# Two adaptive-norm transformer blocks: RMS scaling on another engine, a shorter Newton step, and a later start for the last batches' states

## The chip, the core and the metric

The kernel runs on one core of a Trainium2 chip. A core has five engines, each of which works through its own queue in order: TensorE (PE) for matrix products, with its weight loads (PEld), VectorE (DVE), ScalarE (ACT), GpSimd (POOL) and SyncE (SP), which starts most of the transfers. The metric is the device time in microseconds; before, three runs gave 1119.42, 1120.37 and 1123.93 us, median 1120.37.

## The reference, cut to what matters

The input is 8 sequences of 512 tokens by 128 channels. Block 0 is an attention with 16 heads and then a mixture of eight experts with two chosen per token. Block 1 is a state-space layer and then a second mixture with a small feed-forward. Each half is preceded by a layer norm, scaled and shifted by rows from a modulation, and followed by a gated residual. The change lies in block 1:

```
# state-space layer: depthwise convolution, projection, a scan over 512 tokens
xc    = conv(x) + conv_b
proj  = xc @ Win + b_in                      # delta, B_in, C for 16 states
A_bar = exp(softplus(delta) * A)
h     = scan(A_bar, B_bar)                   # h_t = A_bar_t h_{t-1} + B_bar_t
y     = C * h @ Wout + b_out

# second mixture: all experts, gates that are zero outside the top two
x1       = x + silu(pointwise(causal_conv(x)))
rw       = gates of the two largest logits of x1
ye       = silu(x1 @ expert_w[e] + expert_b[e])           # e = 0..7
r        = x1 + (sum_e rw[e] * ye[e]) @ out_w + out_b
h        = norm_w * (r / sqrt(mean(r * r) + 1e-6))        # RMS norm
out      = h + gelu(h @ ff_down_w + ff_down_b) @ ff_up_w + ff_up_b
```

The 512 tokens of a sequence ("batch" b below) are held as four tiles of 128 tokens.

## The kernel before, in words

The kernel has three phases in one program. Attention runs slot by slot for all batches. Then block 0's mixture runs as a list of n = 62 blocks of 256 tokens (work, lines 1460 to 1464): routed tokens, and the shared expert for everyone. Under these blocks, and then after them, runs block 1.

Block 1's order is written out by hand. when(t, function, arguments) at line 829 puts a call at step t; while blocks are left, one step runs per block, and after them the steps from n on follow each other at once. A step is no time, it is a place in the order: what is issued at a lower step, or at the same step but registered earlier, comes first in the queue of each engine. Every instruction is pinned to that order, so one that waits holds up all that is behind it on its engine.

The steps that matter:

- **States.** The batches go through the state-space layer in groups 0 to 3, 4 and 5, 6 and 7 (GROUPS, line 1131). gather (line 972) fetches the mixture's rows with POOL's indirect transfers; combine (986) adds them with the gates, on DVE; two_stats, ssm_root, ssm_centre, ssm_channels and ssm_conv make the convolved channels; ssm_project (1167) makes the inputs of the states; chain_1 to chain_4 (1195 to 1232) are the state arithmetic of a whole group, with exponentials and a logarithm on ACT, four operations on POOL (da, ts) and the scan on DVE; out_weights (1234) and ssm_out (1241) bring the result back to the tokens.
- **Lead-in.** lead_in (1495) takes one batch from ssm_out through the second layer norm (ffn_root, ffn_centre), ffn_channels, ffn_pointwise, ffn_logits and the choice of two experts (ffn_ranks, ffn_chosen, ffn_tanh, ffn_gates) to ffn_gates_out. There PE transposes the gates, and SP writes them to memory, from where ffn_spread (1341) loads them, repeated over the partitions, as gb. In ffn_ranks POOL multiplies the tie mask rk_eq, on which ffn_chosen waits.
- **Experts.** base[b] (1506) is the step of batch b's first expert, eight steps a batch. At base[b] + e expert_in multiplies (PE) and applies SiLU (ACT, ye); three steps later expert_gate multiplies with the gate (DVE, t), and for some e POOL adds two or four such t; expert_sum (1393) then multiplies by out_w into r.
- **RMS norm.** rms_squares on ACT, rms_root on DVE and POOL, where a power of -1/2 gives a first root; rms_scale (1410) refines the root with one Newton step, root_end (326), and makes h; rms_turn (1417) transposes h, copies it to h2t and makes two small factors for ff_up: diag, the gate of the residual on a diagonal, and the gated feed-forward weights up (in the profile futg). root_end serves the layer norms too.
- **End.** ff_down (1429, with Gelu) and ff_up (1436) for batches 0 to 3, 4 to 6, and 7; ff_up also adds the residual on DVE and starts the output's transfer.

norm_row (1035) spreads the norm's weight over the partitions once, as the row nw that rms_scale uses. It runs at step 11. The scheduling lines that the change moves are 1506, 1530 and 1571 to 1590.

Of the kernel before, what the change touches and what calls it, by code (L numbers as in the profile page):

```python
# [10 lines left out]
FP = mybir.dt.float32  # L11
I32 = mybir.dt.int32
U32 = mybir.dt.uint32
AF = mybir.ActivationFunctionType
ALU = mybir.AluOpType
# [3 lines left out]
B, S, D = 8, 512, 128  # L19
P = 128  # L20
NC4 = S // P
NT = B * NC4
NE, NF = 8, 4
# [45 lines left out]
def tile_adaln_two_blocks(  # L69
# [21 lines left out]
    V, A, G, T, Q = nc.vector, nc.scalar, nc.gpsimd, nc.tensor, nc.sync  # L91

    const = ctx.enter_context(tc.tile_pool(name="const", bufs=1))
    stat = ctx.enter_context(tc.tile_pool(name="stat", bufs=4))
# [3 lines left out]
    def ct(shape, name):  # L98
        return const.tile(shape, FP, tag=name, name=name)
# [10 lines left out]
    ident = ct([P, P], "ident")  # L110
# [29 lines left out]
    fut_sb = ct([32, D], "fut_sb")  # L140
# [4 lines left out]
    def col(name, i=0, n=1):  # L145
        a = COLS[name][0] + i
        return pc[:, a : a + n]
# [34 lines left out]
    mpads = []  # L182
# [10 lines left out]
    mod1 = ct([P, 6, B], "mod1")  # L193
# [5 lines left out]
    with tc.tile_pool(name="ps0", bufs=3, space=PSUM) as ps0:  # L199

        def p0():
            return ps0.tile([P, 4, P], FP, tag="p0", name="p0")
# [3 lines left out]
        for layer, mod in ((0, mod0), (1, mod1)):  # L206
            pm = p0()
            pmv = pm.rearrange("p a b -> p (a b)")
            for k in range(6):
                T.matmul(  # L210
                    pmv[:, 8 * k : 8 * k + 8],
                    lhsT=wmod_sb[:, layer, k * D : (k + 1) * D],
                    rhs=sc_t[:, 8 * layer : 8 * layer + 8],
                    start=True,
                    stop=True,
# [29 lines left out]
        for src, dst in rows:  # L245
            for b0 in range(0, B, 4):
                pg = p0()
# [67 lines left out]
    def root_begin(r, var, eps, scale=None, on=None):  # L315

        on = on or V
        v = stat.tile([P, NC4], FP, tag="var4", name="var4")
        if scale is None:
            on.tensor_scalar(v, var, eps, None, ALU.add)  # L320
        else:
            on.tensor_scalar(v, var, scale, eps, ALU.mult, ALU.add)
        G.tensor_tensor(r, v, mhalf, ALU.pow)
        return v

    def root_end(r, v, on=None):

        on = on or V
        on.tensor_tensor(v, v, r, ALU.mult)
        on.tensor_tensor(v, v, r, ALU.mult)  # L330
        on.tensor_scalar(v, v, -0.5, 1.5, ALU.mult, ALU.add)
        on.tensor_tensor(r, r, v, ALU.mult)


    dram = ctx.enter_context(tc.tile_pool(name="rows", bufs=1, space=bass.MemoryType.DRAM))
# [17 lines left out]
    pin = tc.keep_in_program_order  # L353
    V, A, G, Q = (InOrder(e, pin) for e in (V, A, G, Q))
# [3 lines left out]
    with tc.tile_pool(name="at", bufs=2) as at, tc.tile_pool(name="sc", bufs=4, space=PSUM) as psc, tc.tile_pool(  # L358
        name="mx", bufs=2, space=PSUM
# [13 lines left out]
        def bank(name):  # L373
            return psc.tile([P, NC4, P], FP, tag="sc", name=name)

        def flat(ps):
            return ps.rearrange("p c t -> p (c t)")
# [451 lines left out]
        def when(t, do, *args):  # L829
            events.setdefault(t, []).append(lambda: do(*args))  # L830

        def lt(shape, name, tag=None, bufs=1):
            return lw.tile(shape, FP, tag=tag or name, name=name, bufs=bufs)
# [179 lines left out]
        k1 = {}  # L1013
# [18 lines left out]
            V.tensor_scalar(g, mod1[:, k, :], col(c), None, ALU.mult)  # L1032
            row_tiles(g, fours(dst))

        def norm_row():
            pg = bank("pnw")
            pin(T.matmul(pg[:, 0, :], lhsT=col("norm_w").to_broadcast([P, P]), rhs=ident, start=True, stop=True))
            k1["nw"] = lt([P, D], "nw")
            A.copy(k1["nw"], pg[:, 0, :])

        def states_1():

            rep = lt([16, 8, 16], "rep")
            V.tensor_copy(rep, ident[0:16, 0:16].unsqueeze(1).to_broadcast([16, 8, 16]))
            pr = flat(bank("prep"))
            pin(
                T.matmul(
                    pr[:, 0 : 6 + D], lhsT=rep.rearrange("n b m -> n (b m)"), rhs=ssm_sb, start=True, stop=True
                )
            )  # L1050
            sr = k1["sr"] = lt([P, 6 + D], "sr")
            V.tensor_copy(sr, pr[:, 0 : 6 + D])
            hm = lt([P, 2], "hm")
            V.tensor_reduce(hm, ident.rearrange("p (s h n) -> p h s n", h=2, n=16), AX.XY, ALU.add)
            wop = k1["wop"] = lt([P, 2, D], "wop")
            for h in range(2):
                V.tensor_scalar(wop[:, h, :], sr[:, 6:], hm[:, h : h + 1], None, ALU.mult)

            bias = k1["bias"] = lt([P, 3], "sbias")
            V.tensor_copy(bias[:, 0:1], sr[:, 1:2])  # L1060
            V.tensor_add(bias[:, 1:3], sr[:, 2:5:2], sr[:, 3:6:2])
            V.tensor_scalar(bias[:, 1:3], bias[:, 1:3], 0.5, None, ALU.mult)
            wip = k1["wip"] = lt([P, 3, 2, 32], "wip")
            V.memset(wip, 0.0)
            for h in range(2):
                c = slice(16 * h, 16 * h + 16)
                V.tensor_copy(wip[:, 0, h, c], win_sb[:, 0:16])
                for k in (1, 2):
                    two = win_sb[:, 32 * k - 16 : 32 * k + 16].rearrange("p (n two) -> p n two", two=2)
                    V.tensor_add(wip[:, k, h, c], two[:, :, 0], two[:, :, 1])  # L1070
                    V.tensor_scalar(wip[:, k, h, c], wip[:, k, h, c], 0.5, None, ALU.mult)
# [336 lines left out]
            f["v"] = root_begin(f["rr"], f["ss"], 1e-6, 1.0 / D)  # L1408

        def rms_scale(b):  # L1410
            f = ffn[b]
            root_end(f["rr"], f["v"])
            h2 = f["h2"] = ek.tile([P, NC4, D], FP, tag="h2", name="h2", bufs=1)
            for c in range(NC4):
                V.scalar_tensor_tensor(h2[:, c, :], f["r"][:, c, :], f["rr"][:, c : c + 1], k1["nw"], ALU.mult, ALU.mult)

        def rms_turn(b):
            f = ffn[b]
            pt = bank("ph2")
            for c in range(NC4):  # L1420
                pin(T.transpose(pt[:, c, :], f["h2"][:, c, :], ident))  # L1421
            f["h2t"] = flat(lt([P, NC4, D], "h2t", tag="sh", bufs=B))
            A.copy(f["h2t"], flat(pt))
            f["diag"] = ek.tile([P, D], FP, tag="diag", name="diag", bufs=4)
            V.tensor_scalar(f["diag"], ident, mod1[:, 5, b : b + 1], None, ALU.mult)
            f["up"] = ek.tile([32, D], FP, tag="futg", name="futg", bufs=4)
            V.tensor_tensor(f["up"], fut_sb, mpads[b // 4][0:32, b % 4, :], ALU.mult)

        def ff_down(b):
            f = ffn[b]  # L1430
# [33 lines left out]
        n = len(work)  # L1464
# [10 lines left out]
        when(13, row_tiles, mod0[:, 5, :], fours(sb_rows))  # L1475
        when(14, scaled_rows, 5, "ff_up_b", cb_rows)
        when(10, row_tiles, mod1[:, 5, :], mpads[0:2])
        when(11, norm_row)
        when(23, states_1)
        when(26, states_2)  # L1480
        when(28, pointwise)
# [2 lines left out]
        def later(t, us):  # L1484
            while us > 0:
                us -= 4.0 if t < n else 2.2
                t += 1
            return t

        def chain(h, t, lags):  # L1490
            steps = ((chain_1, 0), (chain_1, 1), (chain_2, 0), (chain_2, 1), (chain_3, 0), (chain_3, 1), (chain_4,))
            for (do, *args), i in zip(steps, lags):
                when(t + i, do, h, *args)

        def lead_in(b, t):

            when(t, ssm_out, b)
            for i in range(2):
                when(later(t, 2 * i + 1) if t >= n else t, two_stats, b, mv4, i)
            for do, us in (  # L1500
                (ffn_root, 4), (ffn_centre, 8), (ffn_channels, 12), (ffn_pointwise, 16), (ffn_logits, 22),
                (ffn_ranks, 24), (ffn_chosen, 28), (ffn_tanh, 30), (ffn_gates, 32), (ffn_gates_out, 36),
            ):
                when(later(t, us), do, b)

        base = [n + 5 + NE * b for b in range(B)]
        for b in range(B):
            t = base[b]
            for e in range(NE):
                when(t + e, expert_in, b, e)  # L1510
        for b in range(B):
            t = base[b]
# [14 lines left out]
            when(late + (4 if b < last else 3), rms_scale, b)  # L1527
            when(late + (6 if b < last else 4), rms_turn, b)

        for bs, t in ((range(4), base[3] + 20), (range(4, 7), base[6] + 20), ((7,), base[7] + 16)):  # L1530
            for b in bs:
                when(t, ff_down, b)
                when(t + 1 + (b - bs[0]), ff_up, b)
# [34 lines left out]

        for k in range(2 * PC[1]):
            when(n - 2 + k // 3, gather, PB[0] + k // 8, k % 8)  # L1570
        when(n, out_weights, 1)
        chain(1, n, (0, 1, 2, 4, 6, 7, 8))
        lead_in(4, n + 10)
        lead_in(5, n + 13)
        for b, t in ((6, n + 1), (7, n + 4)):
            for c in range(NC4):
                when(t + c, combine, b, c)
            when(t + 4, combine, b, NC4)
            for i in range(2):
                when(t + 5 + i, two_stats, b, mv3, i)  # L1580
                when(t + 12 + i, ssm_conv, b, i)
            when(t + 7, ssm_root, b)
            when(t + 9, ssm_centre, b)
            when(t + 10, ssm_bias, b)
            when(t + 11, ssm_channels, b)
        when(n + 16, out_weights, 2)
        when(n + 19, ssm_project, 2, 0)
        chain(2, n + 20, (0, 1, 2, 4, 6, 7, 8))
        lead_in(6, n + 30)
        lead_in(7, n + 37)  # L1590


        LAST = 2 * STEPS + 8
# [36 lines left out]
        ek = ek_cm.__enter__()  # L1630
# [70 lines left out]
```

## Time and profile before

The profiled execution took 1124.82 us in all, its span from first to last instruction is 1123.0 us, and the mean granted clock of TensorE is 0.943 of full speed.

| Engine | busy, us | share of the span |
|---|---|---|
| PE | 1024.6 | 91% |
| PEld | 668.8 | 60% |
| DVE | 665.2 | 59% |
| ACT | 634.2 | 56% |
| POOL | 470.6 | 42% |

A busy time is a sum of instruction spans. Attention ends near 580 us, the mixture of block 0 near 900 us, and the experts of block 1 fill the rest. Most operations of DVE, ACT and POOL carry the same line, 65, as a helper issues them; they are told apart by the tiles they write and read (out<-in). Rows of the parts that the change touches, over the whole execution:

| Operation | engine | count | median, ns |
|---|---|---|---|
| h<-r,rr,nw (128x128) | DVE | 32 | 343 |
| diag<-ident,mod (128x128) | DVE | 8 | 278 |
| futg<-fut_sb,mpad (32x128) | DVE | 8 | 273 |
| sq<-r (128x128, from PSUM) | ACT | 32 | 278 |
| h2t<-ph (128x512, mean) | ACT | 8 | 582 |
| ACT_TABLE_LOAD (mean) | ACT | 17 after 740 us | 1283 |
| rr<-var,mhalf (128x4) | POOL | 8 | 1392 |
| t<-t (128x512) | POOL | 34 | 1270 |
| wo<-wqk,ga_rows (128x128) | POOL | 8 | 457 |
| yg<-y_rows,yrows (gather; mean) | POOL | 64 | 980 |

### The profile page before, as it was taken

How to read it: one execution, taken by the hardware profiler on the slowest of the kernel's cores; microseconds unless marked ns; L12 is line 12 of the kernel's file. 1: busy time of each engine (PE TensorE's matmuls, PEld its weight loads, DVE VectorE, ACT ScalarE, POOL GpSimd, SP SyncE). 2: the span in 40 equal slices, each digit the busy share in tenths (PEclk: the TensorE clock that was granted, in tenths of full speed). 3: DMA queues.
4: the chain of work that ended last, by engine and by line, in shares of the span. 5: the costliest groups of instructions: out<-in, count | busy, mean ns of one | idle time of the engine just before them, and what ended most of it. 6: DMA issues, size and time to landing. Idle time of an engine off the chain costs nothing. (4 is left out here: it accounts for less than half of the span.)

```text
span 1123.0 us, 24186 instructions
## 1 busy us (share of the span) xinstructions
PE 1024.6 (91%) x9540; PEld 668.8 (60%) x9540; DVE 665.2 (59%) x1356; ACT 634.2 (56%) x1378; POOL 470.6 (42%) x723
## 2 busy tenths in 40 slices
PE   5799999999999999999989999859889957878987
PEld 5255555555555555555579999647778624454555
DVE  4377776776777767777421023025767369697563
ACT  1256666676766667676735565324576444555543
POOL 4401223462544546352562033536441374456570
PEclk9689999999999999999989999969989977889899
DMA  9960000000000000000057677411553032233241
GB/s 286 284 191 2 2 1 12 1 28 4 16 16 9 23 5 27 1 27 5 16 156 207 171 210 208 130 33 43 151 146 95 10 105 80 71 95 97 76 147 38
DMA packets 92032, 90.60 MB, mean 81 GB/s; under 512 B 6768, under 2 KB 71352, under 8 KB 91920
## 3 DMA queue, kind: packets, MB, share of 16 engines
q1 hardware_dynamic: 86928, 78.31, 23.8%
q0 software_dynamic: 4688, 9.68, 2.8%
q8 instruction: 75, 1.23, 0.4%
q10 hardware_dynamic: 304, 1.08, 0.3%
q14 instruction: 37, 0.30, 0.1%
HBM read 57.71 MB, written 31.33 MB: 79 GB/s over the span
## 5 line engine op out<-in xcount | busy, mean ns | idle before, releaser
L65 DVE TENSOR_REDUCE mpad<-pm 128x2 f32<-128x1024 f32 x256 | 309.8, 1221 | 136.1 <-PE pm L446 135.4
L65 ACT ACTIVATE es<-ps 128x512 f32<-128x512 f32 x512 | 275.4, 598 | 156.6 <-PE pm L446 111.1
L474 PE MATMUL ps<-qt,kt 32*128 32x512 f32 x1024 | 292.7, 635 | 0.1
L446 PE MATMUL pm<-kt,qt 32*128 32x512 f32 x1024 | 280.9, 664 | 4.5 <-POOL kt L65 2.4
L495 PEld LDWEIGHTS av<-es,vaug 128*32 128x32 f32 x4096 | 104.3, 109 | 94.4 <-ACT part L65 41.7
L495 PE MATMUL av<-es,vaug 128*32 128x128 f32 x4096 | 138.1, 276 | 0.1
L474 PEld LDWEIGHTS ps<-qt,kt 32*128 32x128 f32 x1024 | 95.3, 185 | 61.1 <-issue 33.3
L65 ACT ACTIVATE hid<-ph,bias 128x256 f32<-128x256 f32 x184 | 72.3, 478 | 57.6 <-PE ph L947 53.6
L708 POOL DMA_INDIRECT x_rows<-tok,ux x64 | 64.6, 1009 | 76.1 <-DMA x_rows<-tok,ux 67.4
L958 PEld LDWEIGHTS pyb<-w2b,hid 128*128 128x128 f32 x736 | 90.9, 195 | 5.7 <-ACT hid L65 3.3
L446 PEld LDWEIGHTS pm<-kt,qt 32*128 32x128 f32 x1024 | 79.6, 190 | 24.7 <-DVE mpad L65 11.2
L958 PE MATMUL pyb<-w2b,hid 128*128 128x128 f32 x736 | 91.4, 278 | 2.9 <-ACT hid L65 2.9
L947 PE MATMUL ph<-xt,w1b 128*128 128x256 f32 x368 | 90.9, 392 | 0.0
L65 POOL TENSOR_SCALAR qt<-qf,mask,zero 128x512 f32<-128x512 f32 x32 | 24.7, 773 | 149.0 <-PE pm L446 128.7
L65 DVE COPY xt<-pxt 128x256 f32<-128x256 f32 x46 | 19.4, 421 | 99.7 <-PE pxt L873 91.5
L978 POOL DMA_INDIRECT yg<-y_rows,yrows x64 | 62.8, 980 | 35.2 <-issue 18.1
L947 PEld LDWEIGHTS ph<-xt,w1b 128*128 128x128 f32 x368 | 69.3, 199 | 8.3
L1374 PE MATMUL pe<-x,l1w_sb 128*128 128x512 f32 x128 | 73.1, 680 | 0.5 <-ACT ye L65 0.4
L65 ACT ACTIVATE ye<-pe,pc 128x512 f32<-128x512 f32 x64 | 43.5, 683 | 40.6 <-PE pe L1374 31.9
L65 POOL TENSOR_TENSOR t<-t 128x512 f32<-128x512 f32 x34 | 49.3, 1451 | 36.2 <-DVE t L65 23.8
L65 DVE TENSOR_TENSOR t<-ye,gb 128x512 f32<-128x512 f32 x64 | 53.2, 848 | 4.6 <-POOL t L65 4.6
L958 PE MATMUL pyb<-ws,hid 128*128 128x128 f32 x256 | 36.2, 287 | 12.5 <-issue 12.5
(318 smaller groups left out, 1533.3 us busy)
## 6 DMA issues: line engine op xcount, KB each, us to landing
x_rows<-zeros SPq DMA_DIRECT2D x16, 1024.0 KB
gb<-g_rows SPq DMA_DIRECT2D x32, 512.0 KB
w1b<-in_w1t SPq DMA_DIRECT2D x46, 256.0 KB
w2b<-in_w2t SPq DMA_DIRECT2D x46, 256.0 KB
xg<-x_rows SPq DMA_DIRECT2D x46, 128.0 KB
y_rows<-yb SPq DMA_DIRECT2D x46, 128.0 KB
x<-in_x SPq DMA_DIRECT2D x8, 256.0 KB
h_chan<-hf SPq DMA_DIRECT2D x8, 256.0 KB
```

The costliest lines, as they stand in the source:

```text
L65: return lambda *args, **kwargs: self.pin(call(*args, **kwargs))
L446: T.matmul(pm[:, i, :], lhsT=qt[r : r + 32, qc * P : (qc + 1) * P], rhs=kt[r : r + 32, :], start=True, stop=True,)
L474: T.matmul(ps, lhsT=kt[r : r + 32, kc * P : (kc + 1) * P], rhs=qt[r : r + 32, :], start=True, stop=True)
L495: T.matmul(ps[32 * j : 32 * j + 32, 0, :], lhsT=vaugs[b % 2][:, kc, 4 * j + m, :], rhs=es_of[4 * g + kc, j][:, q], start=(kc == 0), stop=( ...
L708: nc.gpsimd.indirect_dma_start(out=x_rows[h], out_offset=IndirectOffsetOnAxis(ap=chosen["ux", b][:, k, c : c + 1], axis=0), in_=half[h]["t ...
L947: pin(T.matmul(ph[:, f, :], lhsT=it["w1"][:, f * P : (f + 1) * P], rhs=it["x"], start=True, stop=True))
L958: T.matmul(py[:, c, :], lhsT=it["hid"][:, f, c * P : (c + 1) * P], rhs=it["w2"][:, f, :], start=(f == 0 and "shared" not in it), stop=(f = ...
L978: nc.gpsimd.indirect_dma_start(out=gathered[b][:, k, c, :], out_offset=None, in_=y_rows[h], in_offset=IndirectOffsetOnAxis(ap=half[h]["yro ...
L1374: pin(T.matmul(pe, lhsT=l1w_sb[:, 2 + e, :], rhs=x1s[b], start=True, stop=True))
```

## The change

**RMS norm.** The product of r with the root moves from four DVE operations, which also multiplied by the row nw, to four ACT copies with a scale per token. The norm's weight is then applied by channel, as the scale of the copy that takes the transposes to h2t, so norm_row and its row are gone. diag and up move from DVE in rms_turn to POOL in rms_scale, which comes two steps earlier (one for batch 7).

**Newton step.** root_end on DVE takes three operations in place of four and a tile of its own; the tag var4 gets eight buffers in place of four. On POOL it stays as it was.

**Order.** Group 1's chain starts five steps later; combine and what follows it for batches 6 and 7 nine steps later; lead_in of batch 4 four steps later and of batch 5 five; group 2's projection and chain eight steps later; lead_in of 6 and 7 seven steps later. The experts of batches 6 and 7 begin five steps later, so that no expert is issued at steps n+53 to n+57, and ff_down of batches 0 to 3 goes from n+49 to n+53. The gathers keep their steps.

```diff
     def root_end(r, v, on=None):
         on = on or V
+        if on is V:
+            q = stat.tile([P, NC4], FP, tag="var4", name="q4", bufs=8)
+            V.tensor_tensor(q, r, r, ALU.mult)
+            V.scalar_tensor_tensor(q, q, -0.5, v, ALU.mult, ALU.mult)
+            V.scalar_tensor_tensor(r, q, 1.5, r, ALU.add, ALU.mult)
+        else:
...
         def rms_scale(b):
             f = ffn[b]
             root_end(f["rr"], f["v"])
             h2 = f["h2"] = ek.tile([P, NC4, D], FP, tag="h2", name="h2", bufs=1)
             for c in range(NC4):
-                V.scalar_tensor_tensor(h2[:, c, :], f["r"][:, c, :], f["rr"][:, c : c + 1], k1["nw"], ALU.mult, ALU.mult)
+                A.activation(h2[:, c, :], f["r"][:, c, :], AF.Copy, scale=f["rr"][:, c : c + 1])
+            f["diag"] = ek.tile([P, D], FP, tag="diag", name="diag", bufs=4)
+            G.tensor_scalar(f["diag"], ident, mod1[:, 5, b : b + 1], None, ALU.mult)
+            f["up"] = ek.tile([32, D], FP, tag="futg", name="futg", bufs=4)
+            G.tensor_tensor(f["up"], fut_sb, mpads[b // 4][0:32, b % 4, :], ALU.mult)
 
         def rms_turn(b):
...
-            A.copy(f["h2t"], flat(pt))
-            f["diag"] = ek.tile([P, D], FP, tag="diag", name="diag", bufs=4)
-            V.tensor_scalar(f["diag"], ident, mod1[:, 5, b : b + 1], None, ALU.mult)
-            f["up"] = ek.tile([32, D], FP, tag="futg", name="futg", bufs=4)
-            V.tensor_tensor(f["up"], fut_sb, mpads[b // 4][0:32, b % 4, :], ALU.mult)
+            A.activation(f["h2t"], flat(pt), AF.Copy, scale=col("norm_w"))
...
-        base = [n + 5 + NE * b for b in range(B)]
+        base = [n + 5 + NE * b + (5 if b > 5 else 0) for b in range(B)]
...
-        for bs, t in ((range(4), base[3] + 20), (range(4, 7), base[6] + 20), ((7,), base[7] + 16)):
+        for bs, t in ((range(4), base[5] + NE), (range(4, 7), base[6] + 20), ((7,), base[7] + 16)):
...
-        when(n, out_weights, 1)
-        chain(1, n, (0, 1, 2, 4, 6, 7, 8))
-        lead_in(4, n + 10)
-        lead_in(5, n + 13)
-        for b, t in ((6, n + 1), (7, n + 4)):
+        when(n + 8, out_weights, 1)
+        chain(1, n + 5, (0, 1, 2, 4, 6, 7, 8))
+        lead_in(4, n + 14)
+        lead_in(5, n + 18)
+        for b, t in ((6, n + 10), (7, n + 13)):
...
-        when(n + 16, out_weights, 2)
-        when(n + 19, ssm_project, 2, 0)
-        chain(2, n + 20, (0, 1, 2, 4, 6, 7, 8))
-        lead_in(6, n + 30)
-        lead_in(7, n + 37)
+        when(n + 20, out_weights, 2)
+        when(n + 27, ssm_project, 2, 0)
+        chain(2, n + 28, (0, 1, 2, 4, 6, 7, 8))
+        lead_in(6, n + 37)
+        lead_in(7, n + 44)
```

More of the change, by code (lines that the diff above doesn't have):

```diff
@@ L317, in root_begin @@
         on = on or V
-        v = stat.tile([P, NC4], FP, tag="var4", name="var4")
+        v = stat.tile([P, NC4], FP, tag="var4", name="var4", bufs=8)
         if scale is None:
@@ L328, in root_end @@
         on = on or V
[L329 to L332, printed above, removed]
+        if on is V:
[4 more added lines that the diff above has]
+        else:
+            on.tensor_tensor(v, v, r, ALU.mult)
+            on.tensor_tensor(v, v, r, ALU.mult)
+            on.tensor_scalar(v, v, -0.5, 1.5, ALU.mult, ALU.add)
+            on.tensor_tensor(r, r, v, ALU.mult)
     dram = ctx.enter_context(tc.tile_pool(name="rows", bufs=1, space=bass.MemoryType.DRAM))
@@ L1033, in scaled_rows @@
             row_tiles(g, fours(dst))
[L1035 to L1039, printed above, removed]
         def states_1():
@@ L1477, in tile_adaln_two_blocks @@
         when(10, row_tiles, mod1[:, 5, :], mpads[0:2])
-        when(11, norm_row)
         when(23, states_1)
```

## The prediction

> **What bounds it now.** I read the page's slices first, then the timeline of the last 225 us, the busy times by stretch, and single tiles. Up to about 900 us PE is 90% busy or more in nearly all slices, and all that the change touches there is one matmul and one copy. After 900 us PE is nine tenths busy only here and there. The busy times by stretch (start and end, length, PE, weight loads, DVE, ACT, POOL, granted clock, DMA share, GB/s):
>
> ```profile
> 900.00:920.00 20.00, 9.81 (x29) 5.04 (x30) 15.00 (x41) 10.75 (x15) 16.40 (x17) 0.72 0.45 140
> 920.00:940.00 20.00, 12.17 (x36) 7.62 (x36) 16.47 (x50) 5.33 (x11) 7.70 (x7) 0.59 0.20 58
> ...
> 905.00:1016.00 111.00, 82.71 (x312) 47.34 (x310) 88.61 (x209) 55.94 (x113) 62.50 (x62) 0.80 0.29 92
> 1016.00:1099.00 83.00, 72.82 (x336) 44.24 (x336) 52.14 (x114) 42.44 (x94) 46.55 (x36) 0.94 0.32 102
> 1099.00:1123.00 24.00, 17.97 (x117) 13.31 (x115) 9.68 (x30) 7.05 (x17) 2.44 (x2) 0.95 0.16 45
> ```
>
> I cut the tail in three. **Stage 1**, 905 to 1016 us, is the experts of batches 0 to 3 (steps n+5 to n+36); DVE is the fullest engine, 88.6 of 111 us. **Stage 2**, 1016 to 1099, is batches 4 to 7; PE is fullest, 72.8 of 83, DVE only 52. **Stage 3** is the end: the last sums, ff_down and ff_up, with PE fullest. Why PE idles 18 us of the first 40 is in the timeline (start, length, engine, instruction, and in brackets the idle time before it with its releaser):
>
> ```profile
> 911.38 0.73 POOL L65 TENSOR_TENSOR rk_eq<-rk_eq,tri 128x256 f32<-128x256 f32 x1
> ...
> 916.15 1.57 POOL L65 TENSOR_SCALAR da<-dl,asm 32x512 f32<-32x512 f32 x1
> ...
> 921.93 0.74 POOL L65 TENSOR_TENSOR rk_eq<-rk_eq,tri 128x256 f32<-128x256 f32 x1
> 922.70 0.42 DVE L65 TENSOR_TENSOR rk_gt<-rk_gt,rk_eq 128x256 f32<-128x256 f32 x1 [3.92 <-POOL rk_eq L65]
> ...
> 929.64 0.19 DVE L65 SCALAR_TENSOR_TENSOR gate<-rk,z 128x32 f32<-128x32 f32 x1
> ...
> 929.98 1.01 PE L1336 MATMUL pgt<-ident,gate 128*8 128x128 f32 x4 [6.95 <-DVE gate L65]
> ```
>
> PE's order puts batch 3's gate transposes (pgt, step n+10) ahead of more expert matmuls. They wait for the gates, those for the tie mask rk_eq, and that stands on POOL behind gathers and group 1's state work (da, ts). The tile rows (ns, least/median/most) carry the other costs:
>
> ```profile
> L65 DVE SCALAR_TENSOR_TENSOR h<-r,rr,nw x32: 340/343/352, 970.0 to 1112.9; 128x128 f32<-128x128 f32 x32
> L65 DVE TENSOR_TENSOR var<-var,rr x16: 144/164/1228, 968.2 to 1111.5; 128x4 f32<-128x4 f32 x16
> L65 DVE TENSOR_TENSOR t<-ye,gb x64: 671/684/1772, 928.8 to 1103.2; 128x512 f32<-128x512 f32 x64
> ```
>
> A 0.16 us operation that sometimes takes 1.23, and a 0.68 one that takes up to 1.77, were held: at 968.19 two such var steps took 1.41 us while POOL ran a t addition from 967.93 to 969.39.
>
> **The RMS edits.** DVE loses per batch the four h products (1.13 us together at 970.04), one operation of root_end (0.2 us from start to start: 969.63, 969.84), and diag and futg (0.28 + 0.27): 1.9 us. ACT gains four scaled copies from PSUM. No such row exists; the copy nw<-pnw of that size takes 271 ns, and a per-partition operand costs 683 - 598 = 85 ns (ye against es), so 0.36 us each; bounds are 0.27 and 0.48 (xh, two such operands, from SBUF). With sq's 0.4 us spacing the four take 1.2 to 1.7 us. The scaled h2t copy grows from 0.58 to 0.67. ACT is busy 56 of 111 and 42 of 83 us, which hides both. The Trainium skill speaks against it: "ScalarE: Activation LUTs", Rules for kernel authors, sends multiplications to VectorE, and its price there (186 ns + 0.833 per element + 93 for the pointer, an estimate of 386 ns) makes h dearer by 8 x 4 x 0.04 = 1.4 us. The rows say 0.36 against 0.34, as dear, and that the freed engine is stage 1's fullest; I follow the rows.
>
> A wait is added: the copies stand in ACT's queue behind rr from DVE, and the next ye behind them. The gates run three steps behind the ye's, so three results lie ready; I price it at nothing, and at 1 us a batch if DVE runs more than two steps late. The root_ends on DVE before 900 lose 0.2 us each beside a full PE: nothing.
>
> diag and futg go to POOL, 0.45 us each by the wo products (128x128 and 32x128: 457 and 450 ns), between 0.2 (128x4 TENSOR_SCALAR) and 0.8 (128x512). The second rule against the change: "SBUF — State Buffer", SBUF: two separate sides, makes the port pair that POOL shares with DVE an exclusive lock, so 0.9 us a batch could hold DVE for all of it, 7.2 us in sum, where DVE's own rows would make the move a 4.4 us gain. The var and t rows agree that holding happens, but only when a two-input operation meets POOL; I take 1 us in stage 1, nothing later. One new wait: diag has four buffers and is now made at rms_scale, so diag(4) at n+54 must await ff_up(0) in the same step. Behind it on POOL are futg(4) and two t additions (2.5 us) for the sum at n+58; PE has ff_up 1 to 3 meanwhile (3 x 2.2 us), which hides it.
>
> **The moved states, stage 1.** POOL loses four da/ts operations (1.57, 0.70, 1.30, 0.69: 4.3 us) and two wo (0.94) ahead of rk_eq(3), which then comes near 917 instead of 921.9. DVE had 5.2 us between chosen(3) and gates(3) (924.2 to 929.4); now one dl and one gate, 1.4. So pgt(3) can come some 8.5 us earlier. But most of it was no idle time of DVE: while PE stood, DVE did combine(6), combine(7) and chain work that now comes later, so I sum by DVE. Work 88.6; less two h groups 2.3 (970.04 and 1002.83; the third starts at 1018), six saved operations 1.2, diag and futg of two batches 1.1; less two_stats(6), ssm_out(6), centre(6), which leave the stage (1.6 + 0.7 + 0.7); plus 2.5 of chain_1 and combine that ran before 905: 83.5. Idle 22.4, of which 7.0 on rk_eq and 7.3 on dl<-u (the chain behind ACT's table loads and a slow pw triple, 5.36 us at a low clock against 2.74 at full). The first stays, now at about 7.4 since less fills it; the second I halve: 18.7. Sum 102.2, plus 1 for POOL: 103.2, **-7.8**. ACT takes one more table load (5 instead of 4 for chain 1, 1.28 us), beside DVE. POOL's gathers and the gb loads keep their order; on SP the g_rows writes of 6 and 7 go back seven steps, which leaves seven and eight to the first gate product, 16 us or more at 2.3 us a step; batch 7 had about 14 before (write at 1073.7, first product near 1088).
>
> **Stage 2.** Batches 6 and 7 start five steps later, and ff_down and ff_up 0 to 3 fill the gap: 3.6 + 4 x 2.2, with sums 2.1 and transposes and logits 2.2: 16.7 us of PE work, all of it moved and none new. Lower bound -1: the gap costs nothing and some of DVE's relief counts. Upper bound: batch 7's experts, with no ff_up beside them, took 18.8 us (1080.18 to 1098.94); at that pace batches 5 and 6 need 37.6 of the 42.5 they took (1037.63 to 1080.18), so taking ff away returns 4.9 and the gap costs 16.7: +11.8. Nearest rows: PE was busy 18.8 of 20 us at 1060 to 1080 with filler and 16.9 at 1080 to 1100 without; two batches (28 us of PE) without filler lose about 4 to 5, less some 3 to 4 for the 7.5 us that DVE loses (four batches of 1.9). **+1**. In stage 3 PE runs through: 0. norm_row and its copy: 0.
>
> **Sum:** -7.8 + 1 = -6.8 against the profiled execution, 1124.8 (span 1123.0 and 1.8 around it), which lies 4.4 above the median of the runs; against 1120.4 it makes 1113.6, and as the slow pw stretch may shorten too, **1113**.
>
> **Rivals.** (A) The forecast, 1107 to 1118. (B) PE's order decides and not DVE: the 8.5 us of pgt(3) are kept, the slow pw stretch goes (2.6) and the whole dl wait (7.3): -18.4, with stage 2 at -1: 1101. For it: the clock of 0.59 to 0.74 in the stalled stretches. Against: DVE's 80%. (C) Nothing measurable: DVE's deferred work and POOL's longer hold give the first stage's gain back (idle stays 22.4, POOL +3, ACT's wait +1 for two batches): 83.5 + 22.4 + 5 = 110.9, -0.1, with stage 2 at -1: 1119. Moving work between coupled engines speaks for it. (D) Slower: the gap. Expert pace of 2.35 us a step is set by gate products and POOL additions, so PE's filler was free before and now stands alone: +11.8, with the first stage at only -3: 1129. It decides once the first stage gives less than 6.
>
> **Numbers.** A 0.42, B 0.22, C 0.18, D 0.18. Half a per cent is what a measurement can tell here: under 1114.8 lies B and seven tenths of A, 0.51; between, C and the rest of A, 0.31; slower, D, 0.18. The range 1094 to 1129 leaves out B's far end and half of D; A alone has 1107 to 1118.
>
> **To look for.** rk_eq(3) near 917 and pgt(3) near 921; DVE's busy time from n+5 to n+37 about 84 us; four ACT copies of 0.36 us and no wait before them over 1 us; POOL rows of 0.45 for diag and futg; the stretch from batch 5's last expert to batch 6's first near 17 us with PE over 90% busy. The forecast is wrong if DVE idles more than 22 us in stage 1, if ye waits for rr, or if batches 6 and 7 keep 18.8 us each.

## The result, and the profile after

The changed kernel took 1111.05 us (median of four runs, 1110.03 to 1113.11), the kernel before, beside it, 1121.32: ratio 0.9915, 95% interval 0.9897 to 0.9933. Later the kernel before took 1093 to 1095 us in some comparisons and 1122 in others, on the same chip too (last section), so that below times are given as ratios to the kernel before of the same comparison. In a second comparison, where the kernel before took 1093.41, the change's ratio was 0.9958 (0.9944 to 0.9972). The forecast, 1113 against 1120.4, is 0.9934.

The profiled execution took 1111.28 us, span 1109.0, against 1124.82 and 1123.0. Busy time by stretch of the kernel after, the three stages by the first SiLU of batch 4 and the last of batch 7 (columns as in the prediction):

```profile
900.00:1004.00 104.00, 77.55 (x304) 45.13 (x302) 83.42 (x171) 63.72 (x122) 65.75 (x66) 0.85 0.29 93
1004.00:1087.00 83.00, 74.07 (x346) 45.77 (x346) 57.43 (x103) 46.98 (x110) 50.55 (x45) 0.96 0.33 108
1087.00:1109.00 22.00, 17.33 (x113) 12.98 (x112) 6.29 (x15) 9.06 (x24) 4.88 (x6) 0.98 0.17 48
```

The prediction's rows of before end stage 1 at 1016, 2.7 us ahead of batch 4's first SiLU. Cut by the same marks as the kernel after, the kernel before has:

```profile
905.11:1018.73 113.62, 85.21 (x324) 48.77 (x323) 90.79 (x216) 58.57 (x116) 63.95 (x64) 0.80 0.29 94
1018.73:1098.94 80.21, 70.14 (x324) 42.64 (x324) 49.86 (x108) 39.65 (x88) 44.99 (x33) 0.94 0.31 99
1098.94:1123.02 24.08, 18.03 (x118) 13.37 (x116) 9.68 (x30) 7.11 (x18) 2.44 (x2) 0.95 0.15 45
```

Stage 1 has become shorter; VectorE's busy time there fell from 90.8 to some 83.5 us. Stage 2 has not become shorter, and VectorE is busier in it, some 57 against 49.9. The chain of batch 3's gates, in the timeline after:

```profile
911.31 0.74 POOL L65 TENSOR_TENSOR rk_eq<-rk_eq,tri 128x256 f32<-128x256 f32 x1
...
912.08 0.43 DVE L65 TENSOR_TENSOR rk_gt<-rk_gt,rk_eq 128x256 f32<-128x256 f32 x1 [2.54 <-POOL rk_eq L65]
...
915.45 0.19 DVE L65 SCALAR_TENSOR_TENSOR gate<-rk,z 128x32 f32<-128x32 f32 x1
...
916.63 1.06 PE L1336 MATMUL pgt<-ident,gate 128*8 128x128 f32 x4
```

The gate transposes come 13.3 us earlier than before (929.98), and no idle time stands in front of them. 5.1 of the 13.3 us lie ahead of the stage: batch 0's first expert product (pe) starts at 900.05 instead of 905.11. The rows of the moved arithmetic (ns, least/median/most):

```profile
L65 ACT ACTIVATE h<-r,rr x32: 358/367/378, 955.8 to 1098.9; 128x128 f32<-128x128 f32 x32
L65 POOL TENSOR_SCALAR diag<-ident,mod x8: 596/612/2026, 958.8 to 1095.0; 128x128 f32<-128x128 f32 x8
L65 POOL TENSOR_TENSOR futg<-fut_sb,mpad x8: 443/615/937, 959.4 to 1095.6; 32x128 f32<-32x128 f32 x8
```

A VectorE operation that takes far longer than the shortest of its kind was held. The worst are new. Around 920 us, from the timeline after:

```profile
918.77 1.20 POOL L65 TENSOR_SCALAR ts<-ts,small 32x512 f32<-32x512 f32 x1
919.34 4.19 DVE L65 TENSOR_SCALAR bs<-ab,inva 32x512 f32<-32x512 f32 x1
...
919.95 0.86 POOL L65 TENSOR_TENSOR wo<-wop,ga_rows 32x128 f32<-32x128 f32 x2
920.77 1.25 POOL L65 TENSOR_TENSOR t<-t 128x512 f32<-128x512 f32 x1
...
921.99 1.25 POOL L65 TENSOR_TENSOR x<-x,cb_rows 128x512 f32<-128x512 f32 x1
```

bs<-ab,inva took 0.47 us in groups 1 and 2 before. Now it starts beside a run of GpSimd operations and ends only at 923.53, 0.3 us after the last one shown; in group 2 the same happens (3.79 us from 994.40, to 0.3 us after the same addition x<-x,cb_rows).

### The profile page after: what moved, and what is told of

Read it like the earlier page. It is cut to its first block, busy times and chain, and to the rows that moved or that the text cites. A ratio compares the mean times of both kernels' runs of the same rounds, so it can differ in the third digit from the quotient of the medians.

```text
span 1109.0 us, 24143 instructions
## 1 busy us (share of the span) xinstructions
PE 1020.7 (92%) x9538; PEld 667.5 (60%) x9538; DVE 659.2 (59%) x1284; ACT 645.9 (58%) x1411; POOL 480.6 (43%) x739
## 3 DMA queue, kind: packets, MB, share of 16 engines
q1 hardware_dynamic: 86928, 78.31, 24.1%
## 4 chain that ended last, share of the span: by engine, by line
PE 73%; DVE 9%; POOL 5%; ACT 5%; issue 4%; DMA 3%; SPq 1%; another core or an unknown queue 0%; DVEq 0%; ACTq 0%; POOLq 0%
PE ps L480 21%; PE av L501 11%; PE pyb L964 9%; PE ph L953 8%; PE pm L452 4%; PE pmt L468 2%; PE pw L1273 2%; PE r L1362 1%; PE ppt L519 1%; PE pqk L412 1%; DVE xc L65 1%; DVE t L65 1%; DMA x_rows<-tok,ux 1%; DMA x<-in_x 1%; PE pe L1374 1%
## 5 line engine op out<-in xcount | busy, mean ns | idle before, releaser
L1362 PE MATMUL r<-l1w_sb,t 128*128 128x128 f32 x240 | 35.3, 295 | 14.3 <-POOL t L65 11.0
```

The lines of the kernel that those rows point to most:

```text
L1362: T.matmul(ffn[b]["r"][:, c, :], lhsT=x[:, c * P : (c + 1) * P], rhs=w, start=(start and c == 0), stop=stop, skip_group_check=True,)
```

## The experiments

The traces are compared from batch 0's first expert product (pe) on. Stage 1 ends with batch 4's first SiLU, stage 2 with batch 7's last. "Held" is what VectorE's operations took over the shortest of the same operation and tile in all these traces, summed, stages 1 and 2. "Slow pw" counts the products of ffn_pointwise (three for a batch) of the last four batches that took 4.3 to 5.5 us instead of 2.74 to 2.94. Where there are two, one lies in stage 1 (batch 5's) and one in stage 2; a single one lies in stage 2.

| Kernel | before, us | ratio (95%) | stage 1 | stage 2 | end | held | slow pw |
|---|---|---|---|---|---|---|---|
| before, first trace | | | 113.6 | 80.2 | 24.1 | 23.9, 13.7 | 2 |
| before, again | 1122.0 | 1.0004 (0.9988 to 1.0019) | 111.9 | 79.9 | 24.1 | 24.3, 13.7 | 2 |
| after | 1121.3 | 0.9915 (0.9897 to 0.9933) | 104.2 | 82.2 | 22.6 | 27.3, 20.5 | 1 |
| after, again | 1093.4 | 0.9958 (0.9944 to 0.9972) | 105.4 | 82.6 | 22.6 | 26.2, 20.4 | 1 |
| order alone | 1093.4 | 1.0020 (1.0009 to 1.0030) | 105.3 | 88.9 | 24.1 | 27.6, 18.4 | 1 |
| arithmetic alone | 1093.4 | 0.9931 (0.9912 to 0.9950) | 107.4 | 76.4 | 22.6 | 23.6, 15.8 | 1 |
| arithmetic alone, again | 1122.8 | 0.9912 (0.9887 to 0.9938) | 107.4 | 76.2 | 22.6 | 23.5, 15.7 | 1 |
| after, no gap | 1093.4 | 0.9932 (0.9912 to 0.9952) | 114.4 | 71.7 | 23.0 | 23.0, 20.2 | 0 |
| arithmetic, group 1 | 1122.0 | 0.9912 (0.9890 to 0.9934) | 110.1 | 75.0 | 22.9 | 25.6, 15.7 | 2 |
| arithmetic, gap | 1122.0 | 0.9964 (0.9952 to 0.9975) | 110.8 | 78.8 | 22.6 | 22.7, 18.5 | 2 |
| arithmetic, diag on DVE | 1122.0 | 0.9930 (0.9905 to 0.9954) | 111.1 | 77.7 | 22.9 | 23.4, 10.8 | 2 |
| after, bs on ACT | 1122.8 | 0.9978 (0.9967 to 0.9988) | 104.7 | 82.6 | 22.6 | 22.7, 20.9 | 1 |
| arithmetic, h on DVE | 1122.8 | 0.9945 (0.9922 to 0.9968) | 108.6 | 79.3 | 24.2 | 24.5, 12.7 | 1 |
| arithmetic, biases later | 1094.8 | 0.9890 (0.9873 to 0.9906) | 105.3 | 77.5 | 22.9 | 19.6, 19.0 | 1 |

Three pairs of traces tell how far one trace may be trusted: the kernel before twice, the changed kernel twice, the arithmetic alone twice agree within 2 us in each stage. A slow pw in stage 1 goes with some 3 us more there: "arithmetic, gap" has the same order as the arithmetic alone until the stage is over, and takes 110.8 instead of 107.4.

**The change once more, and its two halves.** Order alone is the kernel before with all of the scheduling lines of the diff; arithmetic alone is the changed kernel with all of them undone.

> The changed kernel itself, as the mark for the three that run beside it. If the first measurement holds: ratio to the kernel before 0.9915, at most 0.002 to either side.

> The kernel before with the new order alone (group 1's chain five steps later, combine, statistics, chain and lead_in of batches 6 and 7 later, the gap of five steps before batch 6 with ff_down and ff_up 0 to 3 in it), and the old arithmetic. The forecast's theory, in which VectorE's sum decides the experts of batches 0 to 3: of the -7.8 us there the order brings about 4.2 (3.0 of work that leaves the stage, 3.7 of idle time, less 2.5 that comes in), and the gap costs 1 to 4 without VectorE's relief: -3 us or so, ratio 0.995 to 1.000. Rival B, in which TensorE's order decides: nearly the whole gain, ratio 0.990 to 0.993. If the gap costs what rival D says: above 1.003.

> The kernel before in the old order, with the new arithmetic alone (scaling on ScalarE, the norm's weight in the copy of the transposes, the Newton step in three operations, diag and futg on GpSimd). The forecast's theory: VectorE loses 4.6 us in the stage of batches 0 to 3 and 1 comes back through GpSimd, and in the stage of 4 to 7 little: -3.6 us, ratio 0.996 to 0.998. Rival B: the gates of batch 3 still come late, so nothing: 0.999 to 1.001. If GpSimd's dearer diag and futg (0.61 and 0.45 us in the trace after, and up to 2.0 where held) eat VectorE's relief: 1.001 or more.

The two halves, by stretch (stages 1 and 2 of order alone, then of arithmetic alone in its second trace):

```profile
876.00:981.60 105.60, 81.85 (x306) 47.05 (x304) 88.66 (x192) 62.45 (x115) 63.89 (x62) 0.83 0.28 92
981.60:1070.50 88.90, 77.71 (x343) 47.29 (x344) 61.07 (x131) 41.40 (x94) 45.05 (x35) 0.90 0.31 101
```

```profile
903.00:1011.00 108.00, 80.55 (x328) 45.97 (x326) 86.55 (x195) 61.10 (x126) 68.54 (x71) 0.83 0.31 99
1011.00:1087.00 76.00, 68.35 (x324) 42.38 (x323) 45.12 (x80) 43.80 (x104) 46.51 (x39) 0.96 0.33 105
```

The order brings about the same stage 1 as the whole change, and gives it all back in stage 2, where VectorE's busy time rises to 61 us of 89. The arithmetic alone has a stage 2 of 76 us in which VectorE does 45. In time the order alone costs 0.2%, the arithmetic alone gains 0.7%, and the whole gains 0.4%, which within the intervals is their sum. All three missed what was expected of them. The changed kernel's 0.9958 lies outside 0.9915 with 0.002 to either side. The order alone, 1.0020, lies between what the forecast's theory allowed (1.000) and what rival D needed (1.003), and far from rival B's 0.990 to 0.993. The arithmetic alone, 0.9931, is better than any theory had it (0.996 at best).

> The new arithmetic in the old order once more, beside the two above. If the order adds nothing to it: 0.991 to 0.995, no worse than the changed kernel on a chip where that has 0.9915. If the order carries the gain where the kernel before takes 1120 us: 0.996 or more.

0.9912, no worse than the changed kernel's 0.9915 in another comparison where the kernel before took as long. The order adds nothing there either.

**The gap.** Once taken out of the changed kernel (where group 2's work then also has to start four or five steps earlier), once put alone into the arithmetic in the old order.

```diff
-        base = [n + 5 + NE * b + (5 if b > 5 else 0) for b in range(B)]
+        base = [n + 5 + NE * b for b in range(B)]
-        for bs, t in ((range(4), base[5] + NE), ...
+        for bs, t in ((range(4), base[3] + 20), ...
-        for b, t in ((6, n + 10), (7, n + 13)):
+        for b, t in ((6, n + 6), (7, n + 9)):
...
-        chain(2, n + 28, (0, 1, 2, 4, 6, 7, 8))
-        lead_in(6, n + 37)
-        lead_in(7, n + 44)
+        chain(2, n + 24, (0, 1, 2, 4, 6, 7, 8))
+        lead_in(6, n + 32)
+        lead_in(7, n + 40)
```

> The changed kernel without the gap: batches 6 and 7 follow at once, ff_down and ff_up 0 to 3 stand among batch 4's experts as they did, and group 2's work starts four or five steps earlier than in the changed kernel so that its gates are there in time. The forecast's theory: the gap costs 1 us, and the earlier group 2 brings 3 us of VectorE work back into the first stage: 0.992 to 0.995, no better than the changed kernel. Rival D: the filler was free before, so up to 11.8 us come back: 0.982 to 0.988.

> The new arithmetic in the old order, with the gap alone (batches 6 and 7 five steps later, ff_down and ff_up 0 to 3 in the gap). The forecast's price of the gap, 1 us after VectorE's relief or 4 to 5 without it: ratio 0.994 to 0.997. Rival D, the filler was free among the experts: up to 11.8 us, and from the traces (batch 5 from 28.9 to about 19.5, the gap 17, batch 6 from 14.1 to 11.4) 5 us: 0.997 to 1.002.

Without the gap stage 2 loses 10.9 us and stage 1 gets 9.0 back; the ratio, 0.9932, is as good as the arithmetic alone and a quarter of a per cent better than the change beside it (the intervals just overlap). Alone, the gap makes stage 2 2.5 us longer than it is with the arithmetic alone (78.8 against 76.3), and the ratio is worse than that of the kernel beside it with group 1 moved by 0.005, with intervals that do not overlap. Against all kernels with the arithmetic in the old order (0.9912 to 0.9931) it is worse by 0.003 to 0.005. So the gap costs 2.5 us by the stage and 4 to 6 by the times, which may hold the slow pw of stage 1 as well. That is less than rival D had, and about the 4 to 5 that the forecast gave the gap by itself: its +1 is what VectorE's relief leaves of that, and both kernels compared here have the relief (0.9964 lies in the forecast's 0.994 to 0.997). In the gap TensorE indeed has no idle time, as the stretch of the changed kernel shows:

```profile
1043.00:1061.00 18.00, 18.00 (x110) 12.72 (x109) 10.89 (x18) 9.69 (x18) 10.43 (x10) 1.00 0.27 82
```

**The kernel before with a trace, and group 1 alone.** The second is the arithmetic alone with four of the order's lines (out_weights(1) at n + 8, chain(1, n + 5), lead_in of 4 and 5 at n + 14 and n + 18).

> The kernel before, unchanged, to have its trace beside the others. The first gate product of batch 0 to the end took 217.9 us in the first trace; if that holds on this chip, arithmetic alone (206.4) and the changed kernel (210.6) are to be read against some 215 to 218. Ratio 1.000, at most 0.002 to either side.

> The new arithmetic, and of the new order only group 1's part (out_weights and the chain of batches 4 and 5 and their lead_in four to eight steps later); batches 6 and 7 and ff_down, ff_up as before, no gap. If VectorE's sum decides the experts of batches 0 to 3 (91.5 us of 115 busy with the arithmetic alone), batch 0 gets shorter (36.3 to about 27 us, pgt(3) no longer late) and batches 1 to 3 get it back: ratio 0.991 to 0.995, as with the arithmetic alone (0.9931). If TensorE's order decides, the 8 us of batch 0 stay: 0.985 to 0.989.

0.9912, as the arithmetic alone. Batch 0 gets 3.3 us shorter (33.0 from the first product to batch 1's first SiLU, against 36.3), not 9, and the stage does not get shorter. So this run makes in batch 0 only a third of the difference that it was meant to make. The order alone makes it in full: batch 0 takes 27.1 us against 36.4 in the kernel before, 9.3 less, and of that stage 1 keeps 4 to 5 once the slow pw is taken off. TensorE's order does not decide alone, and rival B's 18 us are out.

**diag and futg back on VectorE.**

```diff
-            G.tensor_scalar(f["diag"], ident, mod1[:, 5, b : b + 1], None, ALU.mult)
+            V.tensor_scalar(f["diag"], ident, mod1[:, 5, b : b + 1], None, ALU.mult)
-            G.tensor_tensor(f["up"], fut_sb, mpads[b // 4][0:32, b % 4, :], ALU.mult)
+            V.tensor_tensor(f["up"], fut_sb, mpads[b // 4][0:32, b % 4, :], ALU.mult)
```

> The new arithmetic in the old order, with diag and futg on VectorE as before (0.28 and 0.27 us a batch there, against 0.61 to 2.0 and 0.45 to 0.94 on GpSimd). The forecast: VectorE gets 1.1 us back in the stage of batches 0 to 3 and GpSimd's hold of 1 us goes: no difference from the arithmetic alone, 0.992 to 0.995. If GpSimd holds VectorE for as long as it works (the rule of the port pair, 1.1 to 1.5 us a batch): 0.988 to 0.992. If VectorE's 0.55 us a batch are what counts in all eight: 0.995 to 0.998.

No difference that the intervals can tell (0.9930 against 0.9912 and 0.9931), as the forecast had it. The held time of stage 2 falls from 15.8 to 10.8 us. How much of that diag and futg did is not shown. With the arithmetic alone the VectorE operations that ran beside one of them were held 3.1 us in stage 2, but only 0.6 us of it with no other GpSimd operation beside them; and with h on VectorE (next) the held time falls too, to 12.7, while diag and futg stay on GpSimd. The time does not show the 5 us: stage 2 took 76.2 to 76.4 us with them held and 77.7 without. TensorE is busy for 68 of the 76 us there.

**h back on VectorE** (by rr alone; the norm's weight stays in the copy to h2t).

```diff
-                A.activation(h2[:, c, :], f["r"][:, c, :], AF.Copy, scale=f["rr"][:, c : c + 1])
+                V.tensor_scalar(h2[:, c, :], f["r"][:, c, :], f["rr"][:, c : c + 1], None, ALU.mult)
```

> The new arithmetic in the old order, with the four h products of a batch on VectorE (by rr alone; the norm's weight stays in the copy of the transposes). If it is VectorE's relief that pays, as the forecast has it (1.13 us a batch, two batches in the stage of 0 to 3, batch 7's on the path at the end): 3 to 5 us of the arithmetic's 7 to 8 go, 0.996 to 0.998. If the arithmetic's gain comes from elsewhere (the three-operation Newton step, diag and futg off VectorE): 0.991 to 0.995, as the arithmetic alone.

Taken alone, 0.9945 lies in the second theory's range; against the 0.9912 beside it, it is 3.7 us more, the first theory's size, with intervals that overlap. The traces are clearer: by stage 1.2, 3.1 and 1.6 us longer, 5.9 in all. So it is mostly VectorE's relief that pays, but not where the forecast had it: most of it lies in stage 2 and at the end. At the end batch 6's four h no longer stand on VectorE ahead of batch 7's last t products, as they do here:

```profile
1091.50 1.13 DVE L65 TENSOR_SCALAR h<-r,rr 128x128 f32<-128x128 f32 x4
1092.54 1.28 DVE L65 TENSOR_TENSOR t<-ye,gb 128x512 f32<-128x512 f32 x2
```

**bs on ScalarE.** Does a held operation decide stage 1?

```diff
-                V.tensor_scalar(bs, held["ab"], -1.0, of_states(h, "inva"), ALU.add, ALU.mult)
+                A.activation(bs, held["ab"], AF.Identity, scale=of_states(h, "inva"), bias=of_states(h, "ninva"))
```

> The changed kernel with one step of the states, bs<-ab,inva (two of 32x512), on ScalarE as a scaled and shifted copy instead of on VectorE. In the traces after, that step took 3.8 and 4.2 us on VectorE where it takes 0.47 in the trace before, while GpSimd ran one operation after the other beside it. If such holds decide the experts of batches 0 to 3: 3 to 7 us less than the changed kernel, ratio 0.985 to 0.989 where the changed kernel has 0.9915 (0.990 to 0.993 where it has 0.9958). If VectorE's next operation is held in its place, or another engine decides: as the changed kernel, within 0.002.

Stage 1 stays as it was, 104.7 us (-inva is made once, as ninva). The timeline shows where group 1's hold went:

```profile
925.93 1.20 POOL L65 TENSOR_SCALAR ts<-ts,small 32x512 f32<-32x512 f32 x1
...
926.51 4.06 DVE L65 SCALAR_TENSOR_TENSOR sh<-yg,gates,sh 128x128 f32<-128x128 f32 x1
```

With bs gone, a later VectorE operation in the queue is held, for 4.06 us instead of 0.32. So the hold stays with the run of GpSimd's operations and not with bs. In the whole stage the held time fell by 4.6 us, from 27.3 to 22.7, and the stage did not get shorter. The ratio is worse for another reason: the edit also moved group 0's bs, ahead of stage 1, where VectorE then waited 7.7 us for ScalarE at bs<-bs,ts (3.2 at bs<-ab,inva in the changed kernel) and TensorE 3.3 for the states (py<-wo,ci; 0.4). From the first transpose of block 1 (ptn) to batch 0's first product it took 139.0 us instead of 133.5.

**GpSimd's additions later.** If GpSimd's runs are the cause, there has to be less of GpSimd in stage 1.

```diff
-            when(t + 5, ffn_bias, b)
+            when(t + 5 if b > 3 else n + 41 + 2 * b, ffn_bias, b)
```

> The new arithmetic in the old order, with GpSimd's additions x<-x,cb_rows of batches 0 to 3 (1.25 us each) put off from their own experts to steps n+41, 43, 45 and 47, into the stage of batches 4 to 7. In the stage of 0 to 3 VectorE was held for 25 us beside 70 us of GpSimd's work, 0.36 us for each. If those holds decide there, 5 us less GpSimd work bring 1.8 us, and up to 5 where GpSimd's queue itself is waited for: 0.987 to 0.990 where the arithmetic alone has 0.9912 (0.989 to 0.992 where it has 0.9931). If the holds fall on other operations or the second stage pays for it: as the arithmetic alone.

0.9890, the best of all kernels here and better than the changed kernel where the kernel before took as long (0.9958; the intervals lie apart). In its one trace the held time of stage 1 fell by 4 us (23.6 to 19.6), where GpSimd had 5.3 us less to do; stage 1 is 2.1 us shorter than with the arithmetic alone, about the 1.8 expected, and stage 2 1.2 longer with 3.2 us more held. From batch 0's first product to the end the trace is 0.8 us shorter; the ratio fell by 0.004, some 4.5 us. The profiled execution was the slowest of its four. The two were not run side by side, and their intervals lie only 0.0006 apart, so how much of it is the four additions stays open.

## Why the prediction was right, and where it was not

The sign and nearly the size were right, the size in part by luck. Where the halves ran side by side, the forecast's theory had the order alone at -3 us, and it took 2.4 more than the kernel before; it had the arithmetic alone at -3.6, and that took 7.1 less. The two errors, some 5 and 4 us, nearly cancel in the sum. By the stages, in the profiled pair: forecast -7.8, +1, 0; measured -9.4, +2.0, -1.6 (against the second trace of the kernel before: -7.7, +2.3, -1.5). The 5.1 us ahead of stage 1 were not forecast; 2.0 of them are there before block 0's mixture makes its first gated bias product (pyb<-b_sb,gt, 708.61 and 706.61), where the change takes away one product and one copy. Kernels with the same work ahead of it started it at 900.0 to 903.3 us where the kernel before, traced again, started at 904.2, so how much of this is the change stays open.

- **VectorE in stage 1: right in sum, wrong in its terms.** 83.5 us of work and 18.7 idle were forecast (19.2 idle by its own terms: the 0.4 us added to the first wait is missing in its sum); 83.4 us are busy and 20.6 idle. With the same cuts before and after, busy time fell by 7.1 us, where 5.1 less 1 for POOL were forecast, and idle time by 2.2, where 3.7 were. Nor is it the work that was summed. Without the held time VectorE's operations fell from 75.5 to 64.0 us, over twice what the forecast took off, and the holds grew from 23.9 to 27.3.
- **rk_eq(3) and pgt(3): right.** 11.3 and 16.6 us after batch 0's first product, where the forecast had 12 and 16.
- **Which half brings stage 1: half right.** Once the second slow pw (some 3 us) is taken off the 112 to 114 us of before, the order shortens it by 4 to 5, as it was given (4.2). The arithmetic alone is worth 1.5 to 3 there, not 3.6, and the order with the arithmetic no more than the order alone.
- **ScalarE's copies: right in cost** (0.367 us, h2t 0.69 against 0.67), **wrong in the wait.** The rows the forecast followed (0.36) were a little nearer than the estimate of 386 ns from the page's price ("ScalarE: Activation LUTs", What ACT_TABLE_LOAD costs). The copies waited for rr six times, 8.1 us in all and 2.9 once, where no wait over 1 us was forecast; with h on VectorE the stages are longer all the same.
- **diag and futg on GpSimd: mis-sized.** 0.60 to 2.03 and 0.44 to 0.94 us instead of 0.45 each. The row near to diag was not the wo product, a TENSOR_TENSOR, though it had the size; GpSimd's TENSOR_SCALAR of that size in the trace before, xh<-x,mv_l0a,rstd_l0a with two columns, took 0.80. The wait of diag(4) came, 1.9 us, and TensorE ran through, as forecast.
- **The step on holding failed.** "Only when a two-input operation meets POOL; I take 1 us in stage 1, nothing later." The trace before already had a one-tensor operation held, up to 1.21 us instead of 0.17:

```profile
L65 DVE TENSOR_SCALAR var<-ss x8: 150/170/1208, 964.8 to 1107.6; 128x4 f32<-128x4 f32 x8
```

In the changed kernel a one-tensor operation was held for 4.19 us, in another a two-tensor one in its place for 4.06, and the held time grew by 3.4 us in stage 1 and by 6.8 in stage 2. From batch 0's first product on, each VectorE operation that was held by more than 0.2 us (44 before, 45 after) has a GpSimd operation beside it. That fits the lock of the Trainium skill ("SBUF — State Buffer", SBUF: two separate sides), by which a VectorE operation with two inputs from the buffer, or in a 2-port mode, and a GpSimd operation exclude each other: the one that starts first has the shared ports for its whole instruction. Which mode the one-tensor operations ran in, the profile does not show. But 4.19 us is longer than any one GpSimd operation beside it (1.44 at most), so the measured hold goes beyond one instruction. That the holds cost the kernel time is not shown: with 4.6 us less of them in stage 1 (bs on ScalarE), or 5 less in stage 2 (diag on VectorE), the stage was no shorter; with 4 less and GpSimd's additions later, stage 1 was 2.1 us shorter.

- **Stage 2: the structure was right, one entry was missing.** 4 to 5 for the gap less 3 to 4 for VectorE's relief made +1. Measured: 2.5 to 6 for the gap, -3.7 for the arithmetic (80.0 to 76.3), both near the forecast. What leaves stage 1 was credited there and never debited here: the states of 6 and 7. With the arithmetic in both, the full order makes stage 2 6 us longer, the gap alone 2.5. The other 3.6 are put down to the moved states, which no run moves alone: with the full order VectorE has 6.2 us more work in stage 2 (39.1 against 32.9 without holds) and is held 4.7 us more.
- **The end: forecast 0, measured -1.6.** The h of batch 6 on ScalarE lie beside batch 7's last t products on VectorE. It made good part of the missing entry.

Of the forecast's signs of being wrong, one came in part: no ye waits for rr itself, but it stands behind the h that do. VectorE's idle time stayed under 22 us. Batch 6 took 11.4 us from its first SiLU to batch 7's and batch 7 13.9 from its first to its last, where it had been 15.6 and 15.5.

Of the rivals, B is out by the order alone; C by the measured ratios, whose intervals leave out 1, though in the second the gain is under half a per cent. D's mechanism exists, at a fifth to a half of its price. What no rival said is that the order as a whole is worth nothing and the arithmetic carries the gain.

## What to carry to other kernels

Whatever a reordering takes out of one stage has to be entered as a cost in the stage it goes to, before its gain is believed: here a gain of 4 us in one stage was a loss of 6 in the next. When one engine holds up another, look for the run of operations that does the holding: to move the one operation that was caught let a later one be caught. Taking work out of the run went with the best ratio here, though how much of that it brought stays open. And run the parts of a change alone: the small edits of the arithmetic, without the larger rearrangement, were as fast as both together.

## What the runs showed that was not expected

The kernel before took 1093.41, 1122.0, 1122.76 and 1094.8 us in four comparisons, the last two on the same chip. In the traces the difference lies in block 0's mixture. In the first trace of before, TensorE's products there come singly, with nothing to wait for that the profile shows; in the changed kernel's second trace 16 of them run as one:

```profile
727.09 0.50 PE L958 MATMUL pyb<-ws,hid 128*128 128x128 f32 x3 [1.83 <-issue]
729.22 0.37 PE L958 MATMUL pyb<-ws,hid 128*128 128x128 f32 x1 [1.63 <-issue]
```

```profile
725.25 2.05 PE L964 MATMUL pyb<-ws,hid 128*128 128x128 f32 x16
```

From the first pyb<-b_sb,gt (708.6 and 706.4 us) to block 1's first transposes (769.6 and 745.4) it took 61.0 and 39.0 us; the arithmetic alone, traced once in each kind of comparison, took 61.0 and 39.1. The DMA records of the traces show one thing beside it. Queue q8, of kind "instruction", brings packets of 16 KiB, 75 in each trace. In the five traces of the short kind one comes every 19 us or so here, at 731.9 to 735.1 among others. In the nine of the long kind none comes for 40 to 42 us, from some 714 to 755, and the single products lie in that stretch. Whether the missing packet makes TensorE wait, or a slower TensorE asks for it later, stays open. The stages of block 1 hardly depend on it (after: 104.2 and 105.4 us, 82.2 and 82.6), but the gain does, 0.85% and 0.42% for the same change. Part of it may lie ahead of stage 1: in the first pair the changed kernel begins the stage 5.1 us earlier, in the second comparison only 1.2 us earlier than the old arithmetic with the new order (875.11 and 876.28). The rest stays open.

The slow pw come at a low granted clock. One in the kernel before, by stretch, with the clock as the third number from the end:

```profile
972.00:977.40 5.40, 5.40 (x8) 2.37 (x9) 2.66 (x4) 0.00 (x0) 2.03 (x2) 0.52 0.25 97
```

The others have 0.50 to 0.65, and 2.74 us at full clock over 5.36 is 0.51. The kernel before has two of them, the changed kernel one: some 3 us of stage 1's gain in the first pair of traces is this. Kernels with the same order in stage 1 had it in some traces and not in others.
